# Attention of a graph network with its first node tiles by slots: one change to a Trainium2 kernel

## The chip, the cores and the metric

The kernel runs on one NeuronCore of a Trainium2 chip, as one program. The metric is the device time of one execution in microseconds (us). Each kernel is run several times; its time is the median. The core has five engines with instruction streams of their own: PE (TensorE, matrix products; its weight loads are listed apart as PEld), DVE (VectorE), ACT (ScalarE), POOL (GpSimd) and SP (SyncE). Transfers go through queues: SP's and ACT's take ordinary loads and stores, POOL's takes the indirect ones, which read (or write) rows at addresses that a column of indices gives.

## What is computed

12500 nodes with 96 features each, 200000 edges sorted by their destination, and 96 features per edge. Four layers follow one another, each with a residual and a layer norm. Cut to what matters:

```python
x = layernorm(x + L0(x, src, dst))      # x W_self + mean of x[src] over dst, times W_neigh
x = layernorm(x + L1(x, src, dst))      # twice: sums of (x W0)[src] over dst, joined with x W1, scaled rows
x = layernorm(x + L2(x, src, dst, edge_attr))
x = layernorm(x + L3(x, src, dst))      # softmax aggregation: exp(relu(x[src])) weights, summed over dst

def L2(x, src, dst, attr):              # 8 heads of 12
    Q, K, V, E = x Wq + bq, x Wk + bk, x Wv + bv, attr We + be
    score = exp(clip(sum_d(K[src] * Q[dst] / sqrt(12) * E), -5, 5))
    return segment_sum(V[src] * score, dst) / (segment_sum(score, dst) + 1e-6)
```

## The kernel before

**Tiles.** Nodes lie in NB = 98 node tiles of 128, edges in NT = 1563 edge tiles of 128, in order of destination. A layer takes rows of a node table at the edges' sources and adds them up at their destinations. There are two ways to do it, and most passes use both side by side.

*By slots.* A node tile owns SQ = 25 groups of 128 slots. Within a group the slots are laid out so that each quarter of 32 takes its rows from one piece of the table, which lies in SBUF. PE gathers with a one-hot product (`granule`; L1299 in the first pass, L1438 later) and sums with a second one (L1313, L1449). The one-hots (`ohT`, `ohd`) are made in the first pass, stored in DRAM (`ohT_d`, `ohd_d`) and loaded again by later passes. Edges that find no slot go to 64 spare slots per node tile, whose rows POOL fetches (L1242, L1251).

*By edges.* `by_edges` takes four edge tiles a unit; POOL fetches the rows of each edge tile from the table in DRAM by an indirect gather (L1383), DVE makes one-hots from the destinations, PE sums (L1369).

**Stages.** `passes` runs them in order:

- The first pass (layer L0): `edge_block` and `edge_steps` (64 edge tiles a step) work out slots and place edges; `expand` makes the one-hots of a node tile; `first_sums` gathers and sums node tiles 0 to NS - 1 = 75 by slots; the other 22 go by edges. The loop over steps in `passes` deals out turns: so many of `first_sums`, and for each so many of `by_edges`.
- Two L1 passes (`whole_pass`): 76 node tiles by slots, 22 by edges, the latter's turns spread evenly over the pass. The last node stage of the second pass computes keys, values and queries and stores them (`kv_d`, float32; `q_d`, two halves in float16).
- The attention (`attention`): all 1563 edge tiles in edge order, in 391 units of four.
- The L3 pass (`whole_pass`): NS3 = 68 node tiles by slots, 30 by edges; its table (`kept[2]`, four float16 parts per feature) stays in SBUF and is filled by the attention's node stages.

**Node stages.** What is done with a finished batch of four node tiles (norms, products with weights, stores) is written as a generator; finished batches wait in `pending`. `advance` moves the oldest one a step; `drain` (L778) does so until none is left, at the end of each pass.

**Order in the attention.** The order of PE, DVE, ACT and POOL there is the order of the code. A step of the loop asks for the gathers of unit u + 8 (`ask`: four gathers of 128 rows of 768 bytes into a `kv` buffer, of which there are 12, L1625), loads unit u + 4 (`fetch`: the edges' features, 192 KB, and the queries, on SP's queue), and computes:

- `score(u)`: PE makes the edge terms `ep` (L1663, eight float32 matmuls) and the destination's queries `qp` (L1667, eight float16 matmuls with the one-hots `ohq`, which ACT makes in `queries`); DVE multiplies them with the keys (L1671, L1672), sums per head and clips (L1674, L1675).
- `weigh(u - 1)`: ACT's exponential (L1683), DVE's product with the values (L1686). After it the kv buffer is free.
- `terms(u - 2)`: two float16 halves of it (ACT L1695, DVE L1696); `one_hots_of(u - 2)`: four one-hots of the destinations on DVE (L1703).
- `scatter(u - 3)`: PE adds up by destination (L1719, about seven matmuls a unit). `done` (from L1732) divides by the weights' sum for each node tile, and every four node tiles a node stage follows (from L1743), of which each step of the loop takes a part.

In the other passes the order across engines follows from the code's order too, with `by_edges` called between batches of slots.

Of the kernel before, what the change touches and what calls it, by code (L numbers as in the profile page):

```python
# [11 lines left out]
F32 = mybir.dt.float32  # L12
# [11 lines left out]
P = 128  # L24
N = 12500
E = 200000
D = 96
# [503 lines left out]
NS3 = 68  # L531
TS = 16 * NS + 8
# [10 lines left out]
def gnn_fast(  # L543
# [67 lines left out]
    kv_d = dram.tile([NB * P, 2 * D], F32, name="kv_d")  # L611
    q_d = dram.tile([(NB + 1) * P, 2 * D], F16, name="q_d")
# [145 lines left out]
    def centred(work, y, n):  # L758
# [3 lines left out]
        nc.vector.tensor_scalar(mean[:, :n], mean[:, :n], 1.0 / D, None, op0=ALU.mult)  # L762
        c = work.tile([P, GB, D], F32, name="centred")
        nc.vector.tensor_sub(c[:, :n, :], y, mean[:, :n, None].to_broadcast([P, n, D]))
# [13 lines left out]
    def drain():  # L778
        while pending:
            advance()  # L780
# [21 lines left out]
    def l0_nodes(work, psum, pieces):  # L802
# [3 lines left out]
        for g, n in node_batches():  # L806
            xg = work.tile([P, GB, D], F32, name="x0", bufs=2)
# [11 lines left out]
            own = work.tile([P, GB, D], F32, name="own0", bufs=2)  # L819
# [32 lines left out]
    def edge_constants(big):  # L852
# [7 lines left out]
        c.first = big.tile([P, NT], BF16, name="first")  # L860
        c.cont = big.tile([P, NT], BF16, name="cont")
        c.same = big.tile([P, NT], BF16, name="same")
# [16 lines left out]
        with tc.tile_pool(name="s_ord", bufs=1) as ordp, tc.tile_pool(name="s_ordp", bufs=2, space=PSUM) as psum:  # L879
# [24 lines left out]
            last = ordp.tile([P, NT], F32, name="last")  # L904
            for j0 in range(0, NT, 512):
                n = min(512, NT - j0)
# [5 lines left out]
            nc.vector.tensor_tensor(c.cont[:, 1:], c.first[:, 1:], last[:, : NT - 1], op=ALU.is_equal)  # L912
# [30 lines left out]
    def edge_block(c, blk, psum, b0):  # L943
# [27 lines left out]
        if slots:  # L971
# [4 lines left out]
            t.rearrange("t (f i) -> t f i", i=4), rowf[:, 1].rearrange("t i f -> t f i"),  # L976
# [65 lines left out]
        b.j = blk.tile([P, BL], F32, name="j")  # L1042
# [7 lines left out]
    def edge_steps(c, work, psum, t0):  # L1050
# [80 lines left out]
        pg_all = pb.rearrange("p k (g i) -> p k g i", i=UE)  # L1131

# [41 lines left out]

    def expand(work, psum, placed, d):
# [3 lines left out]
        p = psum.tile([SQ, P], F32, name="tp")  # L1179
        nc.tensor.transpose(p, lo[:, :SQ], ident)  # L1180
        r = work.tile([SQ, P], BF16, name="lorow", bufs=2)
        nc.scalar.copy(r, p)
        nc.scalar.dma_start(rowd[d], r)
# [158 lines left out]
    def by_edges(of, pool, psum, work, table, done, deep, count=False):  # L1342
# [6 lines left out]
        at = T0 // UE  # L1349
        rows_of = {}  # L1350
        if count:
            ring = [pool.tile([P, UE, W + 2], table.dtype, name=f"rows_e{i}", bufs=1) for i in range(deep)]
            for t in ring:
                nc.gpsimd.memset(t[:, :, W:], 1.0)
# [20 lines left out]
        for d in range(ns, NB):  # L1375
            for k in range(4):
                yield

                while at < min(4 * d - 9 + k + deep, units):
# [17 lines left out]
    def whole_pass(of, table, done, rest_done, at=None):  # L1397
# [6 lines left out]
        with ExitStack() as c2:  # L1404
# [54 lines left out]
            for i in range(0, len(items), 5 * R):  # L1459
# [8 lines left out]
                while made * len(items) < i * 4 * (NB - ns):  # L1468
# [6 lines left out]
            drain()  # L1475
# [509 lines left out]
```

## Time and profile before

| | us |
|---|---|
| Runs of the kernel | 7472.02, 7483.66, 7502.94 (median 7483.66) |
| The profiled execution | 7449.54, of which the span of the core 7447.7 |
| First pass, with what is set up ahead of it | 0 to 1577 |
| First L1 pass | 1577 to 2527 |
| Second L1 pass | 2527 to about 3520 |
| Attention, first unit to last | 3531 to about 6050 |
| L3 pass and the end | 6050 to 7447.7 |

The profiled execution is one more run, 0.5% under the median. Its trace lists every instruction with its start, its duration and what it waited for. A row of a group names the line, the engine, the operation, what is written and read, the count, the busy time, the mean duration of one in ns, and the idle time of the engine ahead of it with what ended that idle time; "issue" there means that the engine waited for nothing that the trace shows. A row of a window gives the busy time and count of each engine within it, the clock that TensorE was granted, the busy share of the DMA engines and GB/s. The list of queues gives packets, MB and the share of the DMA engines' time; q0 is the one of POOL's indirect transfers, q1 those of ordinary loads and stores, q8 and q14 carry instructions to engines.

### The profile page before, as it was taken

What the parts mean: (1) busy time and instruction counts of PE and PEld (TensorE: products, weight loads), DVE (VectorE), ACT (ScalarE), POOL (GpSimd) and SP (SyncE); (2) the same over time, 40 slices, a digit from 0 to 9 for tenths busy, and PEclk for the clock granted to TensorE, in tenths of its full rate; (3) what the DMA queues carried; (4) which work ended last, traced back from release to release, by engine and by line L of the source; (5) the groups of instructions that cost most, each with busy time, mean ns of one, the idle gap of its engine ahead of it and who ended that gap; (6) DMA issues with size and microseconds to landing.
All of it is one profiled execution on the core that took longest, in us unless ns stands there. A gap on an engine that the chain in (4) does not pass through costs nothing.

```text
span 7447.7 us, 155952 instructions
## 1 busy us (share of the span) xinstructions
PE 4699.1 (63%) x63527; PEld 3396.2 (46%) x63527; DVE 4164.5 (56%) x9977; ACT 2805.0 (38%) x5549; POOL 3345.9 (45%) x3338
## 2 busy tenths in 40 slices
PE   5566776746666566666355555555555547777777
PEld 3454554534545444445344444444444434444444
DVE  7577777623434344445466666666666654444545
ACT  2454555523323233333244443444343433333333
POOL 0434444434343344332666565666666643333332
PEclk8677777767777777777555565655555658878888
DMA  4555555443434344444344444444444433333332
GB/s 104 151 163 167 163 167 165 149 116 103 112 99 112 96 110 112 118 119 130 109 129 130 125 131 127 130 132 127 128 130 130 131 90 90 88 88 90 90 89 62
DMA packets 656952, 894.05 MB, mean 120 GB/s; under 512 B 394162, under 2 KB 458885, under 8 KB 651357
## 3 DMA queue, kind: packets, MB, share of 16 engines
q1 hardware_dynamic: 498742, 615.02, 27.2%
q0 software_dynamic: 138784, 262.63, 14.3%
q8 instruction: 500, 8.19, 0.5%
q10 hardware_dynamic: 18695, 6.32, 0.4%
q14 instruction: 231, 1.89, 0.1%
HBM read 747.72 MB, written 135.87 MB: 119 GB/s over the span
## 4 chain that ended last, share of the span: by engine, by line
PE 29%; DVE 22%; another core or an unknown queue 15%; issue 13%; ACT 2%; POOL 1%; DMA 1%; DVEq 0%; ACTq 0%; SPq 0%; POOLq 0%
PE rows L1438 9%; PE acc L1449 7%; DVE ohe L1703 3%; PE acc L1369 3%; DVE s L1672 3%; DVE sc L1674 3%; DVE mh L1696 2%; DVE s L1671 2%; DVE msg L1441 2%; PE ep L1663 2%; PE acc L1719 2%; PE qp L1667 1%; POOL kv L1625 1%; DVE m L1686 1%
## 5 line engine op out<-in xcount | busy, mean ns | idle before, releaser
L1625 POOL DMA_INDIRECT kv<-kv_d,cols x1563 | 1531.4, 980 | 964.3 <-DVE m L1686 464.6
L1438 PE MATMUL rows<-tab,ohT 128*32 128x192 f16 (+1 forms) x21560 | 1114.2, 294 | 696.0 <-issue 610.9
L1441 ACT CAST msg<-rows 128x384 f16<-128x384 f32 (+1 forms) x1440 | 877.2, 641 | 1775.4 <-remote 1041.7
L1441 DVE CAST msg<-rows 128x768 f16<-128x768 f32 x720 | 686.7, 954 | 1478.7 <-remote 1008.1
L1383 POOL DMA_INDIRECT rows_e<-tab_d,cols x1065 | 1105.0, 1038 | 658.9 <-PE acc L1369 349.2
L1438 PEld LDWEIGHTS <-ohT 128*32 128x32 fp8e4 x21560 | 596.2, 101 | 1123.1 <-issue 1044.0
L1449 PE MATMUL acc<-msg,ohd 128*32 128x384 f16 (+1 forms) x10600 | 928.3, 324 | 247.8 <-issue 241.0
L1719 PE MATMUL acc<-mh,ohe 128*128 128x208 f16 x2727 | 516.3, 352 | 844.2 <-DVE ohe L1703 517.8
L1449 PEld LDWEIGHTS <-ohd 128*32 128x32 fp8e4 (+1 forms) x10600 | 554.0, 103 | 526.9 <-issue 434.7
L1719 PEld LDWEIGHTS <-ohe 128*128 128x128 bf16 x2727 | 293.3, 124 | 1011.0 <-DVE ohe L1703 575.5
L1663 PE MATMUL ep<-w_e,attr 97*128 97x96 f32 x3126 | 664.5, 382 | 35.3 <-issue 31.7
L1663 PEld LDWEIGHTS ep<-w_e,attr 97*128 97x128 f32 x3126 | 631.4, 297 | 37.6 <-issue 26.3
L1383 POOL DMA_INDIRECT rows_e<-ex_d,cols x483 | 464.2, 961 | 399.0 <-PE acc L1369 261.9
L1683 ACT ACTIVATE ex<-sc 128x32 f32<-128x32 f32 x391 | 89.7, 229 | 1440.5 <-DVE sc L1675 1166.9
L1303 ACT CAST msg<-rows 128x768 f16<-128x768 f32 x633 | 384.2, 644 | 459.8 <-PE rows L1299 224.6
L1671 DVE TENSOR_TENSOR s<-ep,kv 128x384 f32<-128x384 f32 x391 | 215.6, 551 | 604.7 <-remote 307.1
L1313 PE MATMUL acc<-msg,ohd 128*32 128x194 f16 x7600 | 389.3, 291 | 252.4 <-ACT msg L1303 177.9
L1667 PE MATMUL qp<-qs,ohq 128*128 128x96 f16 x3126 | 352.5, 260 | 292.9 <-issue 270.0
L1667 PEld LDWEIGHTS <-ohq 128*128 128x128 fp8e4 x3126 | 295.4, 136 | 339.4 <-issue 336.4
L1299 PE MATMUL rows<-tab,ohT 128*32 128x192 f16 x7448 | 393.9, 289 | 61.5 <-issue 59.6
L1242 POOL DMA_INDIRECT spare<-tab_d,spare_i x76 | 132.3, 1740 | 656.3 <-PE rows L1299 407.4
L1251 POOL DMA_INDIRECT spare<-tab_d,spare x76 | 72.0, 947 | 731.3 <-PE rows L1438 619.5
(697 smaller groups left out, 7604.9 us busy)
## 6 DMA issues: line engine op xcount, KB each, us to landing
ohT<-ohT_d SPq DMA_DIRECT2D x220, 400.0 KB
ohd<-ohd_d SPq DMA_DIRECT2D x220, 400.0 KB
attr<-cols_edge_attr_dram SPq DMA_DIRECT2D x390, 192.0 KB
bc<-rowd SPq DMA_DIRECT2D x76, 800.0 KB
qb<-qrow SPq DMA_DIRECT2D x97, 512.0 KB
sb<-srow SPq DMA_DIRECT2D x38, 1024.0 KB
ohd_d<-ohd SPq DMA_DIRECT2D x76, 400.0 KB
ohT_d<-ohT SPq DMA_DIRECT2D x76, 400.0 KB
```

The costliest lines, as they stand in the source:

```text
L1299: nc.tensor.matmul(ps[j * GR : (j + 1) * GR, i // R, i % R * W : (i % R + 1) * W], a, b, start=True, stop=True)
L1303: nc.scalar.copy(m[:, : n * R].rearrange("p (b r) t w -> p b (r t) w", r=R)[:, :, :, :D], ps[:, :n, : R * W].rearrange("p b (t w) -> p b t ...
L1313: nc.tensor.matmul(acc[d][j : j + GR, : W + 2], got[d][1][:, q, j : j + GR], m, start=(q == 0), stop=(q == SQ - 1))
L1383: nc.gpsimd.indirect_dma_start(out=m[:, i, :W], out_offset=None, in_=table, in_offset=bass.IndirectOffsetOnAxis(ap=rest_src[:, t : t + 1], ...
L1438: nc.tensor.matmul(ps[j * GR : (j + 1) * GR, i // R, i % R * W : (i % R + 1) * W], a, b, start=True, stop=True)
L1441: (nc.scalar.copy if engine else nc.vector.tensor_copy)(m, ps[:, :, : R * W])
L1449: nc.tensor.matmul(acc[d][j : j + wide, :W], got[d][1][:, q, j : j + wide], m, start=(q == 0), stop=(q == SQ - 1))
L1625: nc.gpsimd.indirect_dma_start(out=kv[:, i, :], out_offset=None, in_=kv_d, in_offset=bass.IndirectOffsetOnAxis(ap=cols[:, t0 + i : t0 + i ...
L1663: nc.tensor.matmul(ep[:, i, :], a[:, i * P : (i + 1) * P], w_e, start=True, stop=True)
L1667: nc.tensor.matmul(qp[:, i, :], ohq[:, i * P : (i + 1) * P], qs[:, t * D : (t + 1) * D], start=(t == 0), stop=(t == 1))
L1671: nc.vector.tensor_mul(s[:, :n, :], ep[:, :n, :], kv[:, :n, :D])
L1719: nc.tensor.matmul(acc[d].rearrange("p t w -> p (t w)"), ohe[:, i, k * P : (k + 1) * P], m[:, i].rearrange("p t w -> p (t w)"), start=(t = ...
```

## The change

1. **Attention of the first MS = 12 node tiles by slots.** The edge tiles that serve only these (184 of them, 46 units) are left out of the edge order: 345 edge units remain. In their place come 75 slot units of four groups (12 x 25 / 4), spread between the 16th edge unit and the 24th from the end. A slot unit gathers keys and values by PE from a float16 table in two halves that lies in SBUF (`kept["kv"]`, from a new `kvh_d`; loaded in 13 pieces of 786 KB, asked for at unit 1): 32 matmuls of 128x192. It makes `qp` as before (8 matmuls), reads its edge terms ready-made from `es_d` (196 KB a unit), and scatters with stored one-hots (4 matmuls), so that it has no kv gather, no `ep` and no L1703. It loads two sets of one-hots (64 KB each) and the rows for `ohq` (128 KB). Spare rows are fetched by POOL once per two node tiles.
2. **What the slot units need is made earlier.** In the first pass `edge_terms` computes `ep` for 198 edge tiles, four at a time (load of 192 KB on ACT's queue, eight float32 matmuls, an ACT copy), and POOL scatters each edge tile to its slots in `es_d` by an indirect write of 128 rows of 384 bytes, one group of four per turn of `first_sums`. `es_d` is filled with zeros first (three writes of 4.9 MB on SP's queue, behind the first three steps). `edge_steps` works out the slots' addresses (11 small DVE operations in each of four steps), and `expand` transposes and stores a second row for node tiles 0 to 11. The last stage of the second L1 pass also makes and stores `kvh_d` (ACT and DVE 128x768, 384 KB, for each of 25 batches).
3. **Weights' sums by fours.** `done` only adds up the two halves; the division is done for four node tiles together in `stage`.
4. **Ends of passes.** `drain(2)` moves two node stages in turn. The turns of `by_edges` are dealt so that they end at 15/16 of a pass.
5. **Loads by steps.** In the passes other than the first, `by_edges` asks at first for fewer units, and for one more (and an eighth) a step, up to the depth it had.
6. **Buffers and order.** kv buffers 12 to 11, accumulators 3 to 2, `s` and `m` 3 to 2, `attr` 6 to 5; `ep` and `qp` share a PSUM tile; the ring of the first pass's `by_edges` 11 to 10. The L3 table is set up only behind the last slot unit; node batches that were finished earlier are stored and loaded back (`bring`, 384 KB each on SP's queue). L3's columns are loaded after the attention. Within an edge tile the edges stand in another order. Centring takes one DVE operation less.

The node tiles' counts NS and NS3 are unchanged. PE's instructions, matmuls and loads taken together with the rest of its stream, go from 127516 to 132734 in the program.

The core of the diff:

```diff
+    def edge_terms(c, work, psum):
+        last = reach(MS - 1)[1]
+        a = c.attr
+        nc.scalar.dma_start(a[:D, : UE * P], cols_attr[:, : UE * P])
+        for t0 in range(0, last + 1, UE):
+            yield
...
+            for i in range(n):
+                nc.tensor.matmul(p[:, i, :], a[:, i * P : (i + 1) * P], w_e, start=True, stop=True)
+            e = work.tile([P, GB, D], F32, name="own0", bufs=4)
+            nc.scalar.copy(e[:, :n], p[:, :n])
...
+            for i in range(n):
+                st = nc.gpsimd.indirect_dma_start(
+                    out=es_d, out_offset=bass.IndirectOffsetOnAxis(ap=c.slot_i[:, t0 + i : t0 + i + 1], axis=0),
+                    in_=e[:, i, :], in_offset=None,
+                )
...
-                while at < min(4 * d - 9 + k + deep, units):
+                steps += 1
+                ahead = 4 * d - 9 + k + deep if count else min(4 * d - 9 + k + deep, start + 3 + steps + steps // 8)
+                while at < min(ahead, units):
...
-                while made * len(items) < i * 4 * (NB - ns):
+                while made * len(items) * 15 < i * 64 * (NB - ns) and made < 4 * (NB - ns):
...
-            drain()
+            drain(2)
...
+            edges = [(t0, min(per, NT - t0)) for t0 in range(first_t, NT, per)]
+            units, made, many = [], 0, MS * SQ // UE
+            for i, e in enumerate(edges):
+                units.append(e)
+                while made < many and (made + 1) * (len(edges) - HEAD - TAIL) <= (i + 1 - HEAD) * many:
+                    units.append((made * UE, None))
+                    made += 1
...
+            def score_slots(u):
...
+                        for t in range(2):
+                            for j, (x, y) in enumerate(pairs):
+                                nc.tensor.matmul(
+                                    kvp[j * GR : (j + 1) * GR, i // 2, i % 2 * 2 * D : (i % 2 + 1) * 2 * D], x,
+                                    y[:, t * 2 * D : (t + 1) * 2 * D], start=(t == 0), stop=(t == 1),
+                                )
...
+                    if u == 1:
+                        kept["kv"] = load_table(tabp, kvh_d)
+                    if u == final:
+                        kept[2] = new_table(tabp, 4 * D, F16)
+                    if u > final + 2 and stored:
+                        bring()
...
+                    if k < MS // 4:
+                        to = es_d[4 * k * SD : 4 * (k + 1) * SD].rearrange("(p r c) w -> p r (c w)", p=P, c=2)
+                        nc.sync.dma_start(to, none[:, None, :].to_broadcast([P, 2 * SQ, 2 * D]))
+                    if k == MS // 4:
+                        next(terms_of)
```

## The prediction

> **What bounds the kernel now.** I read the busy shares first, then the stages as windows, then the waits of the attention, then single runs of gathers. The first two parts of the page say only that nothing is full:
>
> ```profile
> PE 4699.1 (63%) x63527; PEld 3396.2 (46%) x63527; DVE 4164.5 (56%) x9977; ACT 2805.0 (38%) x5549; POOL 3345.9 (45%) x3338
> ...
> q8 instruction: 500, 8.19, 0.5%
> ...
> L1625 POOL DMA_INDIRECT kv<-kv_d,cols x1563 | 1531.4, 980 | 964.3 <-DVE m L1686 464.6
> ```
>
> So stage by stage (columns: length, busy time and count of PE, weight loads, DVE, ACT, POOL, then granted clock, DMA share, GB/s). In order: the first pass, its end, the start of the second L1 pass, the attention, the attention once its last gather is out:
>
> ```profile
> 230.00:1552.00 1322.00, 904.61 (x18358) 671.69 (x18358) 922.66 (x2021) 680.04 (x1085) 558.81 (x431) 0.76 0.51 161
> 1552.00:1577.00 25.00, 9.92 (x61) 6.81 (x61) 12.47 (x41) 3.72 (x13) 0.35 (x1) 0.66 1.00 230
> 2527.00:2596.00 69.00, 14.18 (x114) 6.08 (x115) 2.71 (x6) 3.10 (x6) 45.31 (x48) 0.50 0.31 76
> 3592.00:6020.00 2428.00, 1335.32 (x8693) 1126.62 (x8693) 1559.69 (x4429) 970.19 (x2053) 1485.47 (x1515) 0.58 0.46 128
> 6020.00:6070.00 50.00, 28.28 (x223) 23.07 (x221) 47.42 (x143) 23.31 (x51) 0.00 (x0) 0.72 0.10 28
> ```
>
> The attention's gathers take 2486 us (3531 to 6017) for 391 units of four edge tiles, 6.36 us each. POOL starts gathers 1.25 us apart, so four need 5.0 us per unit. With no gathers left, the last units go by at 4.02 us each (starts of L1696), DVE being busy for 47.4 of 50 us. Gathers are thus the dearer resource, and POOL's waits say why they don't run all the time:
>
> ```profile
> POOL kv L1625 <- DVE m L1686: 464.6, 120, 11.0
> POOL kv L1625 <- issue: 424.3, 1374, 1.3
> ```
>
> 464.6 us are waits for a kv buffer to come free. The cycle is a run of 12 gathers (15 us), then some 4 us of pause: 3 units. What happens to PE meanwhile is seen best at the start of a run and after it, here in the second L1 pass, where PE has other work at hand:
>
> ```profile
> 2603.03:2606.78 3.75, 3.37 (x67) 2.20 (x65) 0.77 (x1) 0.99 (x3) 2.83 (x3) 1.00 0.74 223
> 2606.78:2611.78 5.00, 1.82 (x18) 0.52 (x16) 0.96 (x1) 0.59 (x1) 3.78 (x5) 0.63 0.21 39
> 2611.78:2618.95 7.17, 1.81 (x12) 0.63 (x9) 0.36 (x1) 0.00 (x0) 5.65 (x6) 0.50 0.36 91
> 2621.30:2629.30 8.00, 7.91 (x159) 6.32 (x159) 3.33 (x5) 4.52 (x8) 0.00 (x0) 0.76 0.23 66
> ```
>
> PE gets 132 instructions (matmuls and weight loads) in the first 3.75 us, then 34, then 21, and 318 in 8 us once the gathers stop: 40 a us. So a run of gathers starves PE after its first hundred-odd instructions. An edge unit has 46 (8 ep, 8 qp, 7 scatters, each with its load); three units have 138, more than a run lets through. The first pass has the same thing more mildly, here the run 919.69 to 934.54 and the same time behind it:
>
> ```profile
> 919.69:934.54 14.85, 7.56 (x135) 4.92 (x134) 9.54 (x14) 6.18 (x11) 12.11 (x10) 0.69 0.78 246
> 934.54:949.39 14.85, 10.09 (x278) 8.18 (x281) 12.40 (x37) 9.25 (x14) 3.38 (x2) 0.74 0.54 182
> ```
>
> 143 pairs fewer with 8 gathers more: at 18.7 pairs a us that is 7.6 us, or 0.95 us a gather at worst. Counted in the trace over the whole first pass, PE gets 20 instructions a us where gathers run (431 x 1.25 = 539 us) and about 32 elsewhere: 539 x 12/32 / 431 = 0.47 us a gather.
>
> The q8 line gives a reason: 500 packets of 16.4 KB are 8.19 MB, 64 bytes for each of PE's 127,054 instructions. The Trainium skill ("Runtime: NRT & Kernel Launch", section "Instruction fetch mechanics") says that engines fetch instructions in 16 KiB blocks by a DMA queue of their own, and that crossing a block is "mostly hidden"; by that the new units' 88 PE instructions would cost nothing more. The rows above speak against it where gathers run.
>
> **The change, part by part.** The sum is made on the profiled execution, 7449.5 us (span 7447.7); that is 34 us under the median of the runs, 7483.66, so 34 us are added at the end.
>
> *Attention, removed.* First edge tile 184 instead of 0: 46 edge units go, 184 gathers with them: 46 x 6.36 = **-293**.
>
> *Attention, added.* 75 slot units. Each has 32 row matmuls, 8 qp, 4 scatters, with loads 88 PE instructions, and on DVE what an edge unit has but for the four L1703: 0.55 + 0.55 + 0.55 + 0.19 + 0.55 + 0.58 = 2.98 us. PE, undisturbed: 32 rows at 50 ns (159 in 7.91 us) 1.6; qp 0.84 for eight and scatters 0.18 each, by the spacing of their starts at 6040 to 6044; 3.1 together, so I use 3.0 us a unit for either engine. Without gathers of its own it can lie in POOL's time: 345 x 4.02 + 75 x 3.0 = 1612 us of PE and DVE against 345 x 5.0 = 1725 of POOL. Lower end therefore 0. Upper end: all 88 arrive at the rate of the starved first pass, 269 in 14.85 us: 88 / 18.1 = 4.9 us. The pause of 4 us per cycle holds the 24-odd instructions that a run leaves over, 0.6 us at 40 a us, so it has room for some of the 57 (0.65 slot units) that a cycle now gains; but PE's recovery, the longer wait for a kv buffer (11 instead of 12) and a spare gather that waits for PE six times with gathers queued behind it on POOL take of it. I take half the undisturbed price, 1.5: 75 x 1.5 = +113. Attention **-180** (from -293 to +72).
>
> *Smaller items there.* Weight sums by four tiles: 294 small DVE ops of 0.20 to 0.26 us become 75, about 35 us of DVE that POOL mostly covers: **-5** (0 to -35). The 13 loads of the kvh table (9.6 MB, SP and ACT queues) start at unit 1 and are wanted at unit 16, 100 us later; at 230 GB/s (row 1552) they need 42 us, beside 128 GB/s of the stage: **+5** (0 to 42). The stored groups that come back at the end (22 x 384 KB on SP, in about 150 us) are 56 GB/s on top of 128: nothing; without that room 37. L3's columns are now loaded after the attention; POOL waited 9.0 us for such a load at the attention's start: **+8** (0 to 20).
>
> *First pass.* 50 groups bring 198 scatters on POOL's queue, among its 431 operations and ahead of some edge gathers. No row of before has an indirect write; the nearest is the gather of the same 128 rows in the same stage. Lower end 0: POOL has 763 us free, and a write need not disturb PE as a read does; nothing excludes that. Upper end 198 x 0.95 = 188. I take the stage's mean, 198 x 0.47 = +93. PE gets 8 float32 matmuls a group; L1663 keeps PE busy for 1.7 us for eight (664.5 us over 391 units), 85 us for all; as PE is 68% busy a third stays, +27. The zero fill, 14.7 MB on SP behind the first three steps, lies beside a DMA share of 0.51: nothing; alone it would be 64 us, with the loads of the next one-hots behind it on SP. Together **+120** (0 to 340).
>
> The skill ("DMA: Bandwidth & Descriptors", section "Specifications") gives 512 bytes as the least transfer for line rate, with read-modify-write below; the scattered rows have 384. No run here shows such a write. By that rule I would go to the upper end, 95 us more.
>
> *First L1 pass.* 25 casts of 128x768 on ACT (0.64 us, row L1303) and on DVE (0.95), 25 stores of 384 KB: 40 us beside PE's work, **+10** (0 to 40).
>
> *Ends of passes.* The stretches with little PE work at the ends are 25, 24, 40 and 31 us; in the 40 us two node stages run one behind the other. In turn they overlap, and the edge-order tiles now finish a sixteenth earlier: **-45** (0 to -80). *Starts.* Row 2527: 48 operations of POOL with 114 matmuls in 69 us, and much the same in three passes. POOL now starts with 16 gathers and adds the others step by step. Gathers moved cost again later, where the pass pays 0.9 us or so for 1.25: 20 x 0.35 x 3 = **-20** (0 to -75).
>
> Sum: -180 - 5 + 5 + 8 + 120 + 10 - 45 - 20 = -107: 7342 in the profile's terms, **7377 us** against the median.
>
> **Rivals.**
> *Slot units ride free.* POOL alone paces the attention, -293; the writes disturb PE by half, +60; the rest as above (-47): -280, 7204 us. For it: POOL's 464.6 us wait for DVE, whose four L1703 (1.2 us) slot units don't have. Against: PE's 34 and 21 instructions in 12 us.
> *Given back.* Slot units cost their undisturbed 3.0: -68, +120, -47: 7489 us, no change. For it: PE's work that a run of gathers leaves over is done in the pause now, and 57 more instructions a cycle lengthen it.
> *Slower.* PE's starvation beside POOL's indirect transfers, in both places: scatters at 0.95 us (188 + 27) and slot units at 4.0 (+7): +215 + 7 - 47 = +175, 7659 us. It decides from 75c + first pass over 340 us: with a first pass of 120 from c = 2.9 a slot unit, with 215 from c = 1.7.
>
> **How the numbers follow.** Forecast 0.42, free 0.12, given back 0.22, slower 0.20, else 0.04. About 0.5% (37 us) is what a measurement of this kernel can tell from no change. Faster: most of the forecast's cases, all of the free ones, few of the given-back: 0.54; same 0.18; slower 0.28. The range reaches from the free case's time to two thirds of the way from the given-back case to the slower one: 7205 to 7600. The faster cases alone lie within 7205 and 7446.
>
> **What would show it.** Attention's gathers from 2486 to about 2306 us, with runs of gathers still 12 long; 75 slot units whose matmuls wait for "issue" within the runs would be the starved case. First pass (0 to 1552) longer by 120, with scatters near 1.25 us apart. Ends of passes under 30 us each, starts under 60. I am wrong if the attention gains under 70 or the first pass loses over 200, or if SP's queue, with zero fills ahead of loads, becomes what the first 250 us wait for.

## The result, and the profile after

The changed kernel takes 7712.76 us (median of 4 runs, 7706.57 to 7718.36), the kernel before 7491.8 on the same chip: a ratio of 1.030, 95% interval 1.0282 to 1.0318. It is 221 us slower, where 107 us of gain were forecast. Its profiled execution took 7718.36 us (span 7716.4), 269 more than the one of before; that is 48 more than the medians differ, since the profiled execution of before was a quick one (7449.54 against 7491.8), and in which stages these 48 us lie isn't known.

One thing has to be said ahead of all that follows. The runs were made on several chips, and these are of two kinds for this kernel: on the chip of this comparison and its like (the **first kind**) the kernel before takes 7450 to 7503 us, on three others (the **second kind**) 5308 to 5318. I compare runs within a kind only.

By stages (each from its first gathering product, or the attention from its first gather, to the next one's), in us:

| | before | changed | difference |
|---|---|---|---|
| up to the first sums by slots | 230.1 | 345.5 | +115 |
| first pass from there | 1347.6 | 1510.1 | +163 |
| first L1 pass | 952.1 | 952.1 | 0 |
| second L1 pass | 1001.7 | 1017.5 | +16 |
| attention | 2540.7 | 2508.8 | -32 |
| L3 pass and the end | 1375.6 | 1382.5 | +7 |

Runs shown below leave some stages as they are in the changed kernel, and so show how far one stage varies on the first kind: its first pass ended at 1855.5, 1861.7, 1870.1 and 1874.2 us in four profiles, and its attention took 2499.8 to 2508.8 us in five. Differences of some 20 us in the first pass, and of 10 in the attention, are within that.

The windows of the changed kernel that stand against those shown before (same columns): the stretch up to the first sums, the first pass behind it, its end, the start of the second L1 pass, the attention, and its last units:

```profile
0.00:345.00 345.00, 155.41 (x927) 119.05 (x927) 258.45 (x584) 67.14 (x292) 6.64 (x38) 0.72 0.51 147
349.00:1831.00 1482.00, 972.17 (x18431) 722.87 (x18429) 842.70 (x1883) 699.14 (x1128) 791.61 (x629) 0.73 0.47 149
1831.00:1855.00 24.00, 9.53 (x56) 6.52 (x48) 9.30 (x31) 3.85 (x12) 0.00 (x0) 0.62 1.03 226
2805.00:2874.00 69.00, 24.82 (x322) 14.64 (x323) 6.73 (x10) 7.57 (x12) 42.65 (x46) 0.57 0.38 103
3896.00:6285.00 2389.00, 1461.73 (x10968) 1105.23 (x10968) 1562.33 (x4193) 976.53 (x2198) 1323.78 (x1336) 0.61 0.47 133
6285.00:6335.00 50.00, 28.71 (x197) 22.77 (x201) 46.11 (x133) 23.76 (x51) 0.53 (x1) 0.60 0.21 61
```

See the second row: 18431 matmuls in 1482 us against 18358 in 1322 before. Nearly the same work takes 160 us more, and POOL has 198 operations more in it. These are the writes, dearer in POOL's own time (1.32 us) than an edge gather of the same stage (1.16 us), cheaper than a gather of spare rows (1.54 us); group row of the changed kernel:

```profile
L1213 POOL DMA_INDIRECT es_d<-own,slot_i x198 | 261.4, 1320 | 154.0 <-ACT own L1208 77.7 <-issue 52.7 <-DVE at__15558 L1121 13.2
```

In the attention 46 units are gone, and POOL's waits for a kv buffer have grown by 184 us:

```profile
POOL kv L1733 <- DVE m L1844: 648.9, 147, 10.5
POOL kv L1733 <- issue: 367.6, 1188, 1.5
```

### The profile page after: what moved, and what is told of

It reads as the page before. It is cut to its first block, busy times and chain, and to the rows that moved or that the text cites. A ratio compares the mean times of both kernels' runs of the same rounds, so it can differ in the third digit from the quotient of the medians.

```text
span 7716.4 us, 161464 instructions
## 1 busy us (share of the span) xinstructions
PE 4938.0 (64%) x66165; PEld 3468.5 (45%) x66165; DVE 4179.3 (54%) x9661; ACT 2851.9 (37%) x5769; POOL 3421.3 (44%) x3358
## 4 chain that ended last, share of the span: by engine, by line
PE 35%; DVE 20%; issue 18%; another core or an unknown queue 15%; POOL 4%; ACT 4%; DMA 3%; SPq 0%; ACTq 0%; DVEq 0%; POOLq 0%
PE rows L1490 9%; PE acc L1501 7%; POOL kv L1733 4%; PE acc L1419 3%; DVE msg L1493 2%; PE acc L1362 2%; PE rows L1348 2%; PE acc L1893 2%; DVE ohe L1865 2%; PE eq L1824 2%; DVE mh L1856 2%; DVE sc L1808 2%; DVE s L1832 1%; DVE s L1831 1%
## 5 line engine op out<-in xcount | busy, mean ns | idle before, releaser
L1733 POOL DMA_INDIRECT kv<-kv_d,cols x1379 | 1364.3, 989 | 1046.1 <-DVE m L1844 648.9
L1490 PE MATMUL rows<-tab,ohT 128*32 128x192 f16 (+1 forms) x21560 | 1129.8, 295 | 691.5 <-issue 597.3
L1893 PE MATMUL acc<-mh,ohe 128*128 128x208 f16 x2397 | 471.2, 348 | 421.5 <-DVE ohe L1865 190.9
L1824 PE MATMUL eq<-w_e,attr 97*128 97x96 f32 x2758 | 594.1, 380 | 151.4 <-issue 131.6
L1824 PEld LDWEIGHTS eq<-w_e,attr 97*128 97x128 f32 x2758 | 552.4, 292 | 207.6 <-issue 168.5
L1893 PEld LDWEIGHTS <-ohe 128*128 128x128 bf16 x2397 | 267.7, 127 | 559.8 <-issue 215.2
L1348 PE MATMUL rows<-tab,ohT 128*32 128x192 f16 x7448 | 410.1, 294 | 114.9 <-issue 113.1
L1362 PEld LDWEIGHTS <-ohd 128*32 128x32 fp8e4 x7600 | 221.1, 111 | 349.4 <-issue 333.1
L1831 DVE TENSOR_TENSOR s<-eq,kv 128x384 f32<-128x384 f32 x345 | 190.6, 552 | 338.3 <-remote 183.9
L1419 PE MATMUL acc<-rows_e,ones_e 128*128 128x192 f16 (+2 forms) x2644 | 344.3, 283 | 31.5 <-issue 20.3
```

The costliest lines, as they stand in the source:

```text
L1348: nc.tensor.matmul(ps[j * GR : (j + 1) * GR, i // R, i % R * W : (i % R + 1) * W], a, b, start=True, stop=True)
L1362: nc.tensor.matmul(acc[d][j : j + GR, : W + 2], got[d][1][:, q, j : j + GR], m, start=(q == 0), stop=(q == SQ - 1))
L1419: nc.tensor.matmul(acc[:, : W + count], ones[:, :, i], rows_of[u][:, t % UE + i, : W + count], start=(t + i == first), stop=(t + i == last),)
L1490: nc.tensor.matmul(ps[j * GR : (j + 1) * GR, i // R, i % R * W : (i % R + 1) * W], a, b, start=True, stop=True)
L1733: nc.gpsimd.indirect_dma_start(out=kv[:, i, :], out_offset=None, in_=kv_d, in_offset=bass.IndirectOffsetOnAxis(ap=cols[:, t0 + i - first_t ...
L1824: nc.tensor.matmul(ep[:, i, :], a[:, i * P : (i + 1) * P], w_e, start=True, stop=True)
```

## The experiments

First theory after the comparison: PE starves beside POOL's indirect writes as it does beside gathers, 0.8 us each (the "slower" rival); the first sums come late through the zero fills (A) or the ring that loads of x now share with the rows made from them (B); slot units cost by their PE instructions. SP's queue in the changed kernel speaks for B (start, us, line, transfer): each load of x (L816) goes out behind the stores (L845, L846) of the batch ahead of it.

```profile
305.53 0.37 SPq L845 DMA_DIRECT2D own_d<-own  x1
306.27 0.37 SPq L846 DMA_DIRECT2D tab_d<-tab  x1
306.74 0.49 SPq L816 DMA_DIRECT2D own<-in_x_dram  x1
309.92 0.36 SPq L845 DMA_DIRECT2D own_d<-own  x1
310.66 0.36 SPq L846 DMA_DIRECT2D tab_d<-tab  x1
311.11 0.52 SPq L816 DMA_DIRECT2D own<-in_x_dram  x1
```

### Both kernels on a chip of the second kind

`b0_before`: the kernel before, unchanged. 

> The kernel before, unchanged, for its profile on the chip of these runs. The last four ran on a chip where it takes 5317.6 us instead of 7484. There, in the rows of a kernel close to the changed one, PE gets 35 to 40 instructions in every 1.25 us of a run of gathers, however long, where the first chip's fell to 3. Theory: the two chips differ in nothing but how fast PE gets its instructions while POOL's indirect transfers run. Then this profile has, on a chip like the last, about 5315 us, an attention of about 1950 us (391 units at POOL's 5.0) and a first sum's product at about 236 us; on one like the first, 7450 with stages within 1% of those before.

`a0_after`: the changed kernel, unchanged. 

> The changed kernel, unchanged, for its profile on the chip of these runs. On a chip like the last: the ring shared by the loads of x costs its 104 us at the start there too, the writes about 0.45 us each (90), and the attention gains about 130, so 5400 us against 5317. Rival: without starvation the writes cost nothing (5320). On one like the first: 7710.

Measured: 5310.48 and 5345.24 us. The attention falls from 2040.0 to 1825.7 us, by 214; the first sums come at 227.9 and 345.4; from there the first pass takes 1074.2 and 1170.8; the first L1 pass 542.6 and 562.3. Windows of `b0_before`: first pass, start of the first L1 pass, the rest of that pass, attention:

```profile
228.00:1302.00 1074.00, 795.83 (x18417) 627.08 (x18414) 931.78 (x2061) 679.71 (x1097) 648.42 (x432) 0.84 0.65 203
1302.00:1330.00 28.00, 24.66 (x590) 20.03 (x589) 14.19 (x23) 14.30 (x24) 17.10 (x19) 0.82 0.73 183
1330.00:1840.00 510.00, 457.29 (x9811) 379.75 (x9809) 351.40 (x738) 264.33 (x529) 362.59 (x375) 0.95 0.67 178
2490.00:4390.00 1900.00, 1288.91 (x8437) 1144.18 (x8437) 1543.03 (x4311) 944.36 (x1995) 1452.83 (x1468) 0.57 0.58 159
```

and of `a0_after`: first pass, attention:

```profile
345.00:1516.00 1171.00, 837.84 (x18501) 670.24 (x18501) 850.84 (x1916) 697.37 (x1141) 857.43 (x629) 0.81 0.63 195
2730.00:4440.00 1710.00, 1249.38 (x10842) 990.97 (x10840) 1540.05 (x4136) 965.21 (x2169) 1311.46 (x1309) 0.69 0.67 184
```

In the second row of `b0_before` 590 matmuls run beside 19 operations of POOL in 28 us. The same start of the same pass on the first kind (`before`):

```profile
1577.70:1605.70 28.00, 12.26 (x139) 6.34 (x138) 3.12 (x6) 2.84 (x5) 17.12 (x19) 0.56 0.36 76
```

The same kernel, the same gathers, 139 matmuls instead of 590: no starvation on the second kind. Then gathers pace the attention by themselves (5.2 us for each of 391 units), and slot units are all but free: 391 x 5.22 = 2040, less 46 x 5.22 = 240, and 214 came. The writes do cost here too, and the place is another. PE's waits for spare rows in the first pass, `b0_before` and then `a0_after`:

```profile
PE rows L1299 <- DMA spare<-tab_d,spare_i: 14.9, 2, 8.5
```

```profile
PE rows L1348 <- DMA spare<-tab_d,spare_i: 114.6, 18, 13.4
```

That is 100 us, as much as the 97 that this stretch lost: spare gathers stand behind the writes on POOL's queue. On the first kind PE has no such wait in the first pass, before or changed.

### Start: rings or fills

`a3_fill_behind`:

```diff
+            if g + n == NB:
+                nc.vector.tensor_scalar(zero, own[:, :2, :].rearrange("p g d -> p (g d)"), 0.0, None, op0=ALU.mult)
```

> The changed kernel with the three zero fills of es_d made to wait for the last batch of node rows, so that they are issued behind the loads of x instead of among them. Theory A (the fills hold up the loads of x in the first 150 us): the first sum's product comes at 260 to 280 instead of 349 us. Theory B (the loads of x are held up by the ring that they now share with the rows they become): it stays at 320 to 350, and the fills now stand in the way of the first one-hots instead.

`a4_rings`:

```diff
-            xg = work.tile([P, GB, D], F32, name="own0", bufs=4)
+            xg = work.tile([P, GB, D], F32, name="x0", bufs=2)
...
-            own = work.tile([P, GB, D], F32, name="own0", bufs=4)
+            own = work.tile([P, GB, D], F32, name="own0", bufs=2)
...
-            e = work.tile([P, GB, D], F32, name="own0", bufs=4)
+            e = work.tile([P, GB, D], F32, name="x0", bufs=2)
```

> The changed kernel with the loads of x and the rows made from them in two rings of two buffers each, as before, instead of one ring of four (the edge terms take from the first of the two); the fills stay where they are. Theory B (the shared ring lets a load of x go only behind the rows of the batch ahead of it): the first sum's product comes at 260 to 285 instead of 349 us, and a batch of nodes takes about 5.6 us as before, against 9. Theory A (the fills): it stays above 320.

`a5_rings_fill`: both edits. 

> The changed kernel with the two rings apart and the zero fills behind the last batch of node rows. If the fills cost something of their own behind the ring's 104 us, the first sum's product comes at 231 to 238 us, as before the change, against 245.5 with the rings alone; if they don't, or stand in the way of the first one-hots now, 245 or later.

Measured, all on the second kind, by the first gathering product (some 8 us ahead of the first sum's product that the expectations name): 335.0 (fills moved), 237.8 (rings), 253.9 (both), against 345.4 changed and 227.9 before; whole kernels 5338.83, 5318.47, 5308.92. The ring it is. Moving the fills brings the first sums 10 us forward with the shared ring and puts them 16 us back without, where they stand in the way of the first one-hots (ACT waits 18.3 us for the load of `bc` that they are made from). But of the 108 us at the start only 26 are left at the end of the first pass (1516.2 changed, 1490.6 rings): presumably a late start lets the steps that prepare slots run ahead (not shown), and with rings of two the copies wait for writes, in `a4_rings`:

```profile
ACT x L1208 <- DMA es_d<-x,slot_i: 157.5, 20, 21.6
```

### Writes and products in the first pass

`a1_no_write`: the changed kernel without the `indirect_dma_start` of `edge_terms`. 

> The changed kernel without the 198 indirect writes of the first pass (es_d keeps its zeros, so the first 12 node tiles' attention is computed from zero edge terms); the products, loads and zero fills stay. Theory: the writes starve PE as gathers do, 0.8 us or so each, and are most of what the first pass lost behind its start (349 to 1831, 1482 us, against 1321 before): that stretch falls to 1310 to 1350 us, the start stays at 349, the whole to about 7560. Rival: the products, their loads and the smaller ring of gather buffers take PE's and DVE's time: the stretch stays above 1430.

`a2_no_product`:

```diff
-            p = psum.tile([P, UE, D], F32, name="tp")
...
-            e = work.tile([P, GB, D], F32, name="own0", bufs=4)
-            nc.scalar.copy(e[:, :n], p[:, :n])
...
+            if t0 == 0:
+                e = work.tile([P, GB, D], F32, name="own0", bufs=4)
+                nc.vector.memset(e, 0.0)
```

> The changed kernel with the writes kept, but taking a tile of zeros: no load of edge features, no float32 products and no copies in the first pass (the first 12 node tiles' attention is computed from zero edge terms). Theory (the writes): the stretch behind the start stays within 30 us of 1482. Rival (the products and what they wait for): it falls below 1400.

Measured on the second kind: 5251.77 and 5409.86 us (the kernel before on that chip: 5317.62). Without writes the first pass ends at 1422.8 instead of 1516.2, 93 us or 0.47 us a write; PE's waits for spares are back at 12.5 us. With the writes but no products it ends later, at 1577.3: nothing holds the writes back any more, the last of the 198 is issued at 780 us instead of 1357 (`a0_after`), and PE waits 235.3 us for spares behind them. The products' rival is out on this kind. That writes do more harm in a bunch I had not expected.

The next ones ran on the first kind. `c3_rings_no_write`: rings apart with `e` from each in turn, no writes. 

> The same rings, loads by steps kept, without the 198 indirect writes (the first 12 node tiles' attention is computed from zero edge terms). Theory: writes are all that is left of the first pass's loss once the start is mended; it ends within 25 us of the kernel before's (1302 on a chip like the last, 1578 on the first). Rival: the products, their loads and copies cost 50 us or more beside them.

`c1_rings_steps`: the same rings, writes kept, and

```diff
-                ahead = 4 * d - 9 + k + deep if count else min(4 * d - 9 + k + deep, start + 3 + steps + steps // 8)
+                ahead = 4 * d - 9 + k + deep
```

> The changed kernel with the two rings apart (the edge terms take from each in turn, so that a copy no longer waits for a write two groups back) and without the loads by steps: by_edges asks at a pass's start for all it may, as before. Expected on a chip like the last two: first sum's product at 238 us and the first pass 20 to 60 us shorter than with the rings alone (1490); the first L1 pass back from 562 to 543 us if it is the loads by steps that cost, and still 562 if it is the turns that end at 15/16, which are kept. On one where PE starves: the first L1 pass at 952 either way.

`d4_no_terms`: rings apart, `edge_terms` emptied. 

> The changed kernel with rings apart and no edge terms made in the first pass at all: no loads of features, products, copies or writes (the first 12 node tiles' attention is computed from zero edge terms); zero fills, slots' addresses and second rows stay. On the first chip the kernel with all but the writes ended its first pass at 1657 us, 79 behind the kernel before (1577.7). If those 79 us are the products and their loads, this one ends it at 1578 to 1600; if they are the zero fills and the rest, at 1640 or later. On a chip where PE doesn't starve: 1302 to 1315 against 1302.

`c5_gather`:

```diff
-                    out=es_d, out_offset=bass.IndirectOffsetOnAxis(ap=c.slot_i[:, t0 + i : t0 + i + 1], axis=0),
-                    in_=e[:, i, :], in_offset=None,
+                    out=e[:, i, :].bitcast(F16), out_offset=None, in_=tabs_d[0],
+                    in_offset=bass.IndirectOffsetOnAxis(ap=rest[2][:, t0 + i : t0 + i + 1], axis=0),
```

> The changed kernel with each of the 198 indirect writes replaced by an indirect gather of 128 rows of the same 384 bytes from the first table (the first 12 node tiles' attention is computed from zero edge terms). Theory: a write costs the first pass what a gather does, so its stretch from the first sum to the L1 pass stays within 20 us of the changed kernel's (1171 on a chip like the last, 1510 on the first). Rival: rows under 512 bytes are dearer to write than to read, and the stretch falls by 40 us or more.

The first pass ends at 1577.7 before, 1855.5 changed, 1829.7 with rings and writes, 1657.0 without writes, 1611.2 without any terms, 1882.4 with gathers in place of writes. The whole kernels, of the last four: 7687.93, 7507.93, 7460.04, 7733.55 us. So its loss of 278 us is 26 for the ring, **173 for the writes (0.87 us each)**, 46 for the products with their loads and 33 for the rest, of which the first sums' later start explains 10. Each is a difference of single profiles: the writes are far above the 20 us by which a first pass varies, the products about twice it, the ring and the rest hardly beyond it. My theory allowed the products under 25 and the expectation of `d4_no_terms` put all 79 us there; it is somewhat more than half. Windows of the first pass, `c1_rings_steps`, then `c3_rings_no_write`:

```profile
240.00:1830.00 1590.00, 1006.74 (x18971) 749.17 (x18975) 967.87 (x2127) 708.17 (x1155) 822.29 (x627) 0.73 0.50 154
```

```profile
240.00:1657.00 1417.00, 965.46 (x18959) 731.03 (x18952) 965.13 (x2126) 705.79 (x1155) 567.13 (x428) 0.76 0.54 166
```

Same matmuls but for 12, 199 POOL operations more, 173 us more. What the writes do to PE can be counted in the traces, in the 1.25 us from each indirect transfer's start: beside a write PE starts 19.7 matmuls and weight loads a us in `c1_rings_steps`, beside an edge gather 13.3 (15.6 in `c3_rings_no_write`), and 31 to 33 where no transfer runs. Writes also lengthen the runs: 125 of 626 transfers stand at the ninth place of a run or later, against 59 of 428 (a run being transfers under 1.6 us apart). On the second kind (`a0_after`) it is 32.4 beside a write, 32.7 beside an edge gather and 30.7 elsewhere. So on the first kind writes starve PE as gathers do; an estimate from these rates gives some 130 of the 173 us, (247.5 x 12.3 + 441 x 2.3 + 93 x 1.7) / 32, for the time beside writes, edge gathers and spare gathers. And a gather of the same bytes in the write's place is no cheaper (the first pass ends 27 us later, 8 behind the latest of the four ends given above), so nothing here shows a penalty for writing short rows. `c1_rings_steps` was also to split the smaller parts, but on this kind its first L1 pass takes 954.4 us, as with the loads by steps (952.1).

### The smaller parts alone

`b1_rest`, the kernel before with

```diff
-            drain()
+            drain(2)
...
-                while made * len(items) < i * 4 * (NB - ns):
+                while made * len(items) * 15 < i * 64 * (NB - ns) and made < 4 * (NB - ns):
...
-                while at < min(4 * d - 9 + k + deep, units):
+                steps += 1
+                ahead = 4 * d - 9 + k + deep if count else min(4 * d - 9 + k + deep, start + 3 + steps + steps // 8)
+                while at < min(ahead, units):
```

and the weights' sums by fours. 

> The kernel before with only the smaller parts of the change: weights' sums by fours, two node stages in turn at ends of passes, loads of the edge-order tiles by steps, their turns ended at 15/16; no attention by slots. The prediction gave these -5, -45 and -20, 70 us in all. Theory after the first comparison (first L1 pass 952.1 us before and after, end of the second 41 and 40): they move no stage by over 10 us where PE starves beside gathers, since gathers put off at a start cost as much later; the whole within 15 us of before. Rival: the kvh table's making hid their gain, and this kernel is 40 to 70 us faster.

Measured on the second kind: 5350.49 us, 40 more than `b0_before` (one run of each). The first L1 pass goes from 542.6 to 562.0, the second from 577.4 to 584.4, L3 from 846.6 to 851.4, the attention from 2040.0 to 2044.3: neither theory nor rival, but a loss. Which of the two retimings of `by_edges` costs the 19 us of the first L1 pass was not separated on this kind.

### What a slot unit costs on the first kind

In the slot units' stretch 300 edge units and 75 slot units take 2176 us (starts of L1856). At the 6.36 us that an edge unit took before, a slot unit costs (2176 - 300 x 6.36) / 75 = 3.6 us; at the 6.42 of the 20 edge units ahead of the stretch, 3.3. The undisturbed price was 3.0.

`c4_half`: `for t in range(1)` instead of `range(2)` in the gathering products. 

> The changed kernel with only the high halves of keys and values gathered in the slot units: 16 matmuls with their loads instead of 32, so 56 PE instructions a slot unit instead of 88 (the keys and values of the first 12 node tiles lack their low halves). Theory: where PE starves beside gathers a slot unit costs by its PE instructions, 3.6 us for 88, so 75 x 32/88 x 3.6 = 98 us less attention (2509 to about 2410); where it doesn't starve, slot units lie in POOL's time anyway and nothing changes (1826 within 10). Rival: a slot unit's price is its place in the order (spare gathers, kv buffers), and the attention changes by under 25 us on either chip.

`d1_buffers`, in the kernel before:

```diff
-                kv = uw.tile([P, per, 2 * D], F32, name="kv", bufs=EARLY + 4)
+                kv = uw.tile([P, per, 2 * D], F32, name="kv", bufs=EARLY + 3)
...
-            accp = c2.enter_context(tc.tile_pool(name="e_acc", bufs=3, space=PSUM))
+            accp = c2.enter_context(tc.tile_pool(name="e_acc", bufs=2, space=PSUM))
```

with `s` and `m` at 2 and `attr` at 5. 

> The kernel before with the changed kernel's buffers in the attention and nothing else: 11 kv buffers instead of 12, two accumulators instead of three, two of s and m, five of attr. If the slot units' price of 3.6 us on the first chip is in truth the missing kv buffer, the attention grows here by 150 us or more there (2541 to 2690), for 391 units; theory: under 40 on that chip. On a chip where PE doesn't starve (2040): under 20.

`d2_more_dve`: `for _ in range(3):` ahead of the slot unit's first product on DVE. 

> The changed kernel with the first product on DVE made three times in each slot unit (the same result thrice): 75 x 2 x 0.555 = 83 us more of DVE. Theory for the first chip: gathers and the other engines' work take turns there, so that a slot unit's work lies in the pauses of POOL and its longest engine, DVE, is paid in full: the attention grows by 60 to 90 us (2509 to about 2585). Rival: the slot unit's price is latency or the starved PE, DVE has time between, and it grows by under 30. Where PE doesn't starve (1826) DVE is near its limit as well (4.0 us a unit of 5.0): 10 to 60.

`d3_empty`: `score_slots` returns the places alone, and the scatter takes a tile of zeros. 

> The changed kernel with slot units emptied: their loads and four scatters of a tile of zeros stay, while the gathering products, the queries, and all of DVE's and ACT's work for them go (the first 12 node tiles' attention is zero). Theory: the attention falls by what slot units cost on the chip beside the loads: on the first one by 3.0 to 3.6 us each, 225 to 270 us (2509 to 2240 to 2285); where PE doesn't starve by under 60 (1826 to over 1766). Rival: what they cost is their loads and their place in the order, and it falls by under 100 on the first chip too.

Measured on the first kind (whole kernels 7712.62, 7484.58, 7793.65, 7632.73 us): the attention takes 2485.6 us with half the gathering products (-23, not -98), 2573.0 with the smaller buffers in the kernel before (+32), 2567.6 with 83 us more of DVE (+59), 2413.0 with slot units emptied (-96, not -225 or more). As the changed kernel's attention varies by 9 us, half the products may save as little as 14. And `d1_buffers` as a whole is no slower than the kernel before on its chip (7484.58 against 7503.32); its +32 is taken against the one profile of before (7449.54), and is a ceiling rather than a price. POOL's waits in `c4_half` and in `d3_empty`:

```profile
POOL kv L1733 <- DVE m L1844: 613.4, 137, 10.2
```

```profile
POOL kv L1735 <- DVE m L1821: 455.8, 77, 11.4
```

My theory of PE instructions falls: 32 fewer of 88 should have saved over a microsecond a unit and saved 0.3. DVE's work is paid at 0.7 of its length, so for the most part it seems to lie in pauses of POOL. All the unit's work together is 1.3 us of the 3.6, the buffers 0.4 at most; the rival of `d3_empty` has it, the rest, some 1.9 us or more, is loads or place.

`f1_bare`: slot units without loads, spare gathers or work, four scatters of a constant. 

> The changed kernel with slot units reduced to their place in the order: no loads, no spare gathers, no work but four scatters of a constant tile (the first 12 node tiles' attention is zero). Gathers of the attention, first to last: 2485.8 us before, 2454.6 changed, 2358.7 with the slot units emptied but their loads left, on the first chip. 345 edge units at the 6.45 us of the kernel with 11 kv buffers would be 2225. Theory: the 134 us between are the slot units' loads (34 MB, some of them in rows of 384 bytes, and the buffers that SP's queue waits for), and it falls to 2220 to 2270. Rival: they are the steps that an empty unit takes in the pipeline of the loop, in which the edge units behind it come a step later, and it stays above 2320. On a chip where PE doesn't starve: 1725 to 1800 by either.

`f2_bare_end`: the same, behind all edge units. 

> The same bare slot units, all put behind the last edge unit, so that the 345 edge units run one after the other. Gathers, first to last, on the first chip: 2200 to 2240 by the loads' theory, like the run with bare units among the others; by the rival (steps in the pipeline) also 2200 to 2240, but 80 us or more under that run. If it stays above 2300, neither holds, and the edge units themselves have become dearer, by something else that the change does in the attention.

These two were to tell loads from place, and the chip was of the second kind: 5336.94 and 5377.42 us, gathers from first to last 1801.5 and 1786.0 us, against 1805.1 in `a0_after`. They settle the second kind instead: what the 75 slot units load and compute costs the gathers 4 us there, all together. On the first kind **loads against place stays open**, and with it about half of a slot unit's price.

## Why the prediction was wrong

The forecast was -107 us in the profile's terms, and 269 came: 376 us apart. The price of a slot unit makes 155 of them (at 3.6 us), the writes' 80, the ends and starts 65, and the other items of the first pass 78 (ring 26, products 19, rest 33). The prediction's own signs of being wrong, an attention that gains under 70 and a first pass that loses over 200, both came true (32 and 278).

- *Which price of a write.* The second largest miss: between 0 and 0.95 us I took the stage's mean, 0.47. It measured 0.87 on the first kind, 173 us in place of 93. The mean was of a stage with short runs (324 of its 431 transfers stand at the first to fourth place of a run, 29 at the ninth or later), and the writes lengthen them (110 of 629 in the changed kernel); the run shown beside it gave 0.95. Oddly 0.47 is the price on the second kind, by another mechanism (spares queued behind writes).
- *Products in the first pass.* +27, measured 46; by its own count 85 was the most.
- *The ring.* The prediction weighed buffers only in the attention and missed that one ring of four for loads and results orders each load behind the batch ahead of it: 105 of the 115 us at the start (the first sums come at 240.3 in `c1_rings_steps`), of which 26 stay. The zero fills, which it named as what might go wrong, move the first sums by 10 to 16 us.
- *Slot units.* The step that failed most: 1.5 us taken, 3.3 to 3.6 measured, above the "undisturbed" 3.0, so -32 instead of -180. The reason given (the pause has room for half of a unit's work) was wrong: the waits for a kv buffer grow (464.6 to 648.9 us), and 83 us more of DVE's work cost 59. They also come oftener: one for 9.4 gathers (1379 and 147) instead of 13.0 (1563 and 120), so the runs "still 12 long" didn't come either; with the buffers alone it is 12.7 (`d1_buffers`, 123 waits), with slot units emptied 17.9. But the unit's work explains only 1.3 us of its price, and what the other half is stays open. "Slot units ride free" was right in mechanism for the second kind, by luck: the prediction knew of no such chip.
- *Ends and starts.* -45 and -20, measured nothing on the first kind (on the second `b1_rest`, with the sums by fours, cost 40). The stretches from a pass's last sum by slots to the next stage (for the last pass, to the end) are 25, 22, 41 and 31 us before, and 25, 23, 40 and 32 after. At starts PE does get more (322 matmuls in 69 us instead of 114, in the second L1 pass), and the first L1 pass still takes 952.1 us: what a start gains is lost later in the pass. The 0.35 us taken as gain for each gather put off should have been nothing.
- *kvh, L3's start.* kvh +10, measured +16: right in size. L3's start +8: the L3 pass is 7 us longer, but it varies by as much by itself (1375.6 and, in `d1_buffers`, 1383.6 with the old order; 1377.5 to 1385.6 with the new), so this isn't shown.
- *The rival "slower"* (+175: scatters at 0.95, slot units at 4.0) comes nearest, at 7659 against 7713, and its condition (75c + first pass over 340) was met: 268 + 278 = 546. For the writes its mechanism is borne out too; for the slot units, where it names PE's starvation, `c4_half` speaks against it.
- *The range.* 7600 as its end left out most of that rival's own case. The two starved rows shown were the best evidence there was, and the forecast took half of their price in two places.
- *Instruction blocks.* The q8 reading ("a reason") isn't borne out. In the run of gathers shown, PE executes 55 instructions in 12.2 us, and the DMA view of the kernel before has one instruction packet, 256 instructions, in that time:

```profile
q8 instruction: 1, 0.02, 0.5%
```

The trace shows a trickle of 0 to 10 per 1.25 us from the run's fourth gather on. And the blocks come no later where PE is slow: counted at each landing over the whole kernel before, 256 times the packets landed less the PE instructions started has a median of 12 on the first kind and of -16 on the second (its zero is arbitrary, as the first blocks were there when the trace began). The Trainium skill's sentence ("Runtime: NRT & Kernel Launch", section "Instruction fetch mechanics") that crossing blocks is mostly hidden is thus not contradicted by these rows, and the prediction was wrong to say that they speak against it. Nor is it the granted clock: in the first three of the four rows of the second L1 pass it falls from 1.00 to 0.50, PE's rate from 35 instructions a us to 3. What slows PE beside gathers on the first kind stays open.

The Trainium skill's figure on transfers under 512 bytes ("DMA: Bandwidth & Descriptors", section "Specifications") would have moved the forecast the right way by 95 us. `c5_gather` doesn't show the reason, though: reads of the same 384 bytes cost the pass no less.

## What to carry to other kernels

When the profile shows two engines that take turns (PE's instruction rate falls to a tenth within a run of gathers), price the work that is added in full, not by the room that an average leaves. Here an indirect write cost its stage what a gather costs there, and on the second kind its place on POOL's queue mattered as much as its count. Give loads and results rings of their own, and check a retiming of loads by the length of the whole pass, not by its start.

## What the runs showed of the hardware

Chips ran one and the same program in 7450 to 7503 us or in 5308 to 5318. The difference lies in every stage with runs of indirect transfers (up to the first sums, where there are few, it is 230.1 and 227.9 us): the first L1 pass takes 952.1 or 542.6 us with the same 10400 matmuls (granted clock 0.76 and 0.94). In the first pass PE gets 29 to 40 instructions in the 1.25 us of each of a run's first twelve indirect transfers on the second kind (means by place in the run, `a4_rings`); on the first kind (before) 38 beside the first and 3 from the ninth on. The change is slower by 3.0% on the one kind and by 0.7% on the other (5345.24 against 5307.77, one run each); with rings apart and the fills moved it draws level there (5308.92). No version of the change that computes everything came out ahead of the kernel before on either kind.
